# Scores of the second attention in a two-layer kernel: 32-key instead of 64-key tiles on the matmul array

## The chip, the cores and the metric

The kernel runs on one core of a Trainium2 chip. The metric is the time of one execution on the device, in microseconds (us); 1 us is 1000 nanoseconds (ns). Before the change it takes 3774.46 us, the median of three runs (3773.48 to 3776.23). The profiled execution, from which all views below are taken, spans 3772.0 us.

Names of the engines: PE is the matmul engine, PEld its loading of weights (the stationary operand of a matmul, which is loaded by an instruction of its own), DVE the vector engine, ACT the scalar engine with the exponentials, POOL the general-purpose engine, SP the engine that starts most transfers. SBUF is the on-chip memory, PSUM the small memory that matmuls write to[...].

## What is computed

The input x has 16 images of 256 channels by 32 x 32 positions, so 1024 positions ("tokens") of 256 channels for each image. Two layers follow each other, all in fp32.

The first is a self-attention with 4 heads of width 64, an output projection and a residual. The second is a transformer block: group norm, self-attention with 8 heads of width 32 and a projection, a residual, group norm again, and an MLP from 256 to 1024 channels and back with a GELU.

The part that matters here is the second attention, cut to its core:

```python
q, k, v = qkv[0], qkv[1], qkv[2]                  # each (B, 8 heads, 1024, 32)
attn = jnp.einsum('bhnd,bhmd->bhnm', q, k) * scale + phys_bias
attn = jax.nn.softmax(attn, axis=-1)
out = jnp.einsum('bhnm,bhmd->bhnd', attn, v)
```

The score of query n and key m is a sum over only 32 products (d). A score matrix has 1024 x 1024 entries for each head and image.

## The kernel before, in words

The kernel goes through the images one after the other. For each it runs attention_a (the first attention), then attention_b (the second), then the two halves of the MLP. What does not depend on the attention that is running, such as the next image's query, key and value products (qk_a, v_a), this image's own (qk_b, v_b), or the second half of the previous image's MLP (tile m, the function reduce), is cut into pieces, and a list `fill` says after which step of attention_b which pieces are issued. So in attention_b the PE's instructions come in a fixed order, written out by the program: a unit of scores, the weighting of the previous unit's exponentials with the values, one or two filler pieces, and again.

**A unit of scores** (function `scores`) belongs to an item i (one block of TB = 512 queries and one group of four heads; four items for each image) and to two blocks of 128 keys (m = 0 and 1). For each of the four heads g and each block of 128 keys it writes a 128 x 512 piece of the transposed scores to PSUM: keys on the partitions, queries along the free axis. The head's 32 channels are the rows of the array that the matmul uses (its contraction), the keys are the columns. A head takes 32 of the 128 rows, so four heads fit above each other. Before the change, the 128 keys are split in two halves of HALF = 64, so a matmul uses a tile of 32 rows by 64 columns, and eight such tiles fill the array. That is 16 matmuls in a unit. The trace records each fp32 matmul as two weight loads and two matmuls, so there are 32 matmul records in a unit, and with 16 images x 4 items x 4 units = 256 units, 8192 records.

**Where scores go.** For m = 0, heads 0 and 1 go to two single PSUM banks (tags b0, b1), and heads 2 and 3 to one "wide" buffer of two banks. For m = 1 two wide buffers are used. There are three wide buffers, handed out in turn, also to the fillers. A buffer is free again when ACT or DVE has read it. ACT takes the exponential of each buffer (line 483), DVE sums the exponentials for the denominators (line 498).

**The weighting** (function `weigh`, line 519) multiplies the values with the exponentials of the previous unit: full 128 keys as contraction, 32 output channels of a head as columns, so a tile of 128 rows by 32 columns, four of which fill the array: 8 matmuls, 16 records. The fillers are issued through `product` (line 279), which in attention_b is set by `cols[0] = D` to the same shape, four column tiles of 128 x 32. The denominators (line 541) have this shape too. So in attention_b the scores alone use another tile shape.

The first attention has scores and weighting in tiles of 64 x 64 (lines 336 and 357), and the first MLP product uses the whole array, 128 x 128 (line 802).

## Time and profile before

| what | value |
|---|---|
| time | 3774.46 us |
| span of the profiled execution | 3772.0 us |
| PE busy | 3757.8 us (100%), 38335 matmul records |
| weight loads (PEld) busy | 1492.0 us (40%) |
| DVE, ACT, POOL busy | 2231.3 (59%), 2034.8 (54%), 78.5 us (2%) |
| granted PE clock | full speed over the span |
| data moved | 78.27 MB, mean 21 GB/s |

A record of a matmul in the profile has a start, which is measured, and an end, which is modelled. Matmuls are pipelined: on different tiles of the array they run at the same time, and the next on the same tile starts before the modelled end of the last. So the time for which a group of matmuls holds the engine is read from the spacing of starts, or from the chain of waits, which follows the work that ended last and gives each stretch of it a length. A record's own duration is longer than that and can't be summed.

In the list of groups, a line has the source line, the engine, the operation, output and inputs by their names, the tile of the array (rows*columns) and shape, the count, then the busy time in us and the mean of one in ns, then the idle time of the engine ahead of it and who ended it.

### The profile page before, as it was taken

Reading aid. Unit: us, or ns where it says so; the run is one execution under the profiler, and the core shown is the slowest. Engines: PE = TensorE matmul, PEld = TensorE weight load, DVE = VectorE, ACT = ScalarE, POOL = GpSimd, SP = SyncE. Lnnn points to the kernel's source line nnn. Section 1 sums busy time; section 2 is a strip of 40 time slices with the busy share of each in tenths; the row PEclk is TensorE's granted clock in tenths of the full one; section 3 lists DMA queues with packets and bytes.
Section 4 is the critical chain, followed back from the end, with each engine's and each line's share of the span. In section 5 each row is a group of like instructions: output and inputs, shape, how many; then the busy total and the mean of one; then the engine's idle time right before and its main releaser. Section 6 shows DMA issues by size and latency. Waiting matters only on the chain.

```text
span 3772.0 us, 86793 instructions
## 1 busy us (share of the span) xinstructions
PE 3757.8 (100%) x38335; PEld 1492.0 (40%) x38335; DVE 2231.3 (59%) x2764; ACT 2034.8 (54%) x2624; POOL 78.5 (2%) x245
## 2 busy tenths in 40 slices
PE   9999999999999999999999999999999999999999
PEld 3334343343433434334343333443334333343335
DVE  4674656656566565665656656565565655646573
ACT  4665546555465554555555455554655546555461
POOL 1000000000000000000000000000000000000000
PEclk9999999999999999999999999999999999999999
DMA  2000000000001000000000000010010100000000
GB/s 85 13 13 13 30 13 16 27 13 30 12 17 32 7 30 13 19 29 9 28 13 23 26 10 33 7 33 15 13 30 7 33 15 13 30 7 22 15 12 22
DMA packets 63052, 78.27 MB, mean 21 GB/s; under 512 B 35820, under 2 KB 37356, under 8 KB 62668
## 3 DMA queue, kind: packets, MB, share of 16 engines
q1 hardware_dynamic: 59964, 71.85, 6.2%
q8 instruction: 302, 4.95, 0.5%
q0 software_dynamic: 400, 0.41, 0.1%
q14 instruction: 82, 0.67, 0.1%
q10 hardware_dynamic: 2304, 0.40, 0.1%
HBM read 54.28 MB, written 17.56 MB: 19 GB/s over the span
## 4 chain that ended last, share of the span: by engine, by line
PE 97%; DVE 1%; issue 1%; ACT 1%; DMA 0%; ACTq 0%; POOLq 0%; POOL 0%; DVEq 0%
PE s_b L468 13%; PE acc_b L519 12%; PE m L802 12%; PE m L279 12%; PE s_a L336 12%; PE acc_a L357 11%; PE qk_b L279 6%; PE qk_a L279 6%; PE o L279 3%; PE v_b L279 3%; PE v_a L279 3%; PE j L279 3%; PE den_b L541 1%; PE den_a L388 1%; DVE es_a L369 0%
## 5 line engine op out<-in xcount | busy, mean ns | idle before, releaser
L483 ACT ACTIVATE e_b<-s_b 128x1024 f32<-128x1024 f32 (+1 forms) x1280 | 982.6, 864 | 471.0 <-PE s_b L468 471.0
L498 DVE TENSOR_TENSOR es_b<-es_b,e_b 128x1024 f32<-128x1024 f32 x768 | 899.9, 1220 | 337.5 <-ACT e_b L483 337.5
L344 ACT ACTIVATE e_a<-s_a 128x1024 f32<-128x1024 f32 x512 | 521.4, 1025 | 359.6 <-PE s_a L336 349.2
L468 PE MATMUL s_b<-q,k 32*64 32x512 f32 x8192 | 535.8, 601 | 4.0 <-DVE res_b L532 3.3
L336 PE MATMUL s_a<-q,k 64*64 64x512 f32 x4096 | 532.6, 593 | 1.1
L357 PE MATMUL acc_a<-e_a,v 64*64 64x512 f32 x4096 | 528.5, 589 | 0.0
L369 DVE TENSOR_TENSOR es_a<-es_a,e_a 128x1024 f32<-128x1024 f32 x384 | 469.3, 1222 | 85.4 <-ACT e_a L344 73.3
L519 PE MATMUL acc_b<-e_b,v 128*32 128x512 f32 x4096 | 492.1, 598 | 0.0
L279 PE MATMUL m<-g,w 128*32 128x256 f32 (+1 forms) x7664 | 464.1, 379 | 0.0
L802 PE MATMUL m<-gn_h,w 128*128 128x512 f32 x1024 | 451.3, 595 | 0.3 <-DVE gn_h L692 0.3
L810 ACT ACTIVATE g<-m,m1b 128x512 f32<-128x512 f32 x256 | 176.0, 687 | 358.2 <-PE m L802 358.2
L279 PEld LDWEIGHTS m<-g,w 128*32 128x32 f32 (+1 forms) x7664 | 276.7, 112 | 216.8 <-issue 41.9
L468 PEld LDWEIGHTS s_b<-q,k 32*64 32x64 f32 x8192 | 174.2, 130 | 288.8 <-issue 147.1
L802 PEld LDWEIGHTS m<-gn_h,w 128*128 128x128 f32 x1024 | 192.2, 190 | 230.6 <-issue 229.8
L357 PEld LDWEIGHTS acc_a<-e_a,v 64*64 64x64 f32 x4096 | 161.9, 133 | 277.5 <-issue 236.1
L336 PEld LDWEIGHTS s_a<-q,k 64*64 64x64 f32 x4096 | 152.6, 133 | 278.1 <-issue 211.7
L519 PEld LDWEIGHTS acc_b<-e_b,v 128*32 128x32 f32 x4096 | 108.5, 109 | 351.1 <-ACT e_b L483 194.7
L532 DVE TENSOR_TENSOR res_b<-res_b,acc_b 128x512 f32<-128x512 f32 x192 | 131.1, 683 | 196.2 <-PE acc_b L519 196.2
L279 PE MATMUL qk_b<-gn_g,wq 128*32 128x512 f32 (+1 forms) x1280 | 234.0, 592 | 0.0
L279 PE MATMUL qk_a<-x,wp 128*32 128x512 f32 (+1 forms) x1856 | 231.3, 592 | 2.1 <-ACT q L715 1.5
L736 DVE TENSOR_TENSOR v<-v_b,eones 128x512 f32<-128x512 f32 x64 | 44.0, 688 | 291.2 <-PE v_b L279 291.2
L498 DVE TENSOR_TENSOR es_b<-e_b,e_b 128x1024 f32<-128x1024 f32 x128 | 150.6, 1218 | 0.0
(121 smaller groups left out, 2096.3 us busy)
## 6 DMA issues: line engine op xcount, KB each, us to landing
rd_a<-row_a SPq DMA_DIRECT2D x64, 256.0 KB
out_dram<-x SPq DMA_DIRECT2D x64, 256.0 KB
rd_b<-row_b SPq DMA_DIRECT2D x252, 64.0 KB
x<-in_x_dram SPq DMA_DIRECT2D x30, 512.0 KB
w<-in_L_conv_mlp_w_dram SPq DMA_DIRECT2D x2, 1024.0 KB
x<-in_x_dram SPq DMA_DIRECT2D x4, 256.0 KB
sp_b<-d_b SPq DMA_DIRECT2D x63, 8.0 KB
row_b<-inv_b SPq DMA_DIRECT2D x63, 8.0 KB
```

What stands on the lines that cost most here:

```text
L279: nc.tensor.matmul(o[sl], w[:, sl], r, **flags)
L336: nc.tensor.matmul(s[h : h + HALF, g, :], kT[g * D : (g + 1) * D, c, kb * P + h : kb * P + h + HALF], qT[g * D : (g + 1) * D, c, t * TB : ...
L344: nc.scalar.activation(e, s, AF.Exp, scale=float(D) ** -0.5)
L357: nc.tensor.matmul(accs[i][h][g * D : (g + 1) * D, :], v[h * HALF : (h + 1) * HALF, kb, c * 2 + g], e[h * HALF : (h + 1) * HALF, g, :], st ...
L369: nc.vector.tensor_add(sums[i], held[i] if kb == 1 else sums[i], e)
L468: nc.tensor.matmul(outs[g][h : h + HALF, :], kT[g * D : (g + 1) * D, c, k0 : k0 + HALF], qT[g * D : (g + 1) * D, c, t * TB : (t + 1) * TB] ...
L483: nc.scalar.activation(to, s, AF.Exp, scale=float(D) ** -0.5)
L498: ins = nc.vector.tensor_add(d, es[n] if kb == 0 else d, es[2 * block + n])
L519: nc.tensor.matmul(acc[g * D : (g + 1) * D, :], v[:, kb + m, c * G + g], es[2 * m + g // 2][:, g % 2, :], start=(m == 0), stop=(m == 1),)
L532: nc.vector.tensor_add(r, r, acc)
L802: nc.tensor.matmul(ps, k["w1"][:, cc, hc * P : (hc + 1) * P], hn[0][:, cc, t * TB : (t + 1) * TB], start=(cc == 0), stop=(cc == CC - 1),)
L810: nc.scalar.activation(g, ps, AF.Gelu, bias=k["m1b"][:, hc : hc + 1])
```

## The change

In `scores`, the loop over the keys of a block steps by D = 32 instead of HALF = 64. Each head's 128 keys are then four tiles of 32 rows by 32 columns instead of two of 32 by 64. Sixteen such tiles fill the array. The column width becomes that of the weighting, the denominators and the fillers around it; the rows stay 32.

```diff
                 for g in range(G):
-                    for h in range(0, P, HALF):
+                    for h in range(0, P, D):
                         k0 = (kb + m) * P + h
                         nc.tensor.matmul(
-                            outs[g][h : h + HALF, :],
-                            kT[g * D : (g + 1) * D, c, k0 : k0 + HALF],
+                            outs[g][h : h + D, :],
+                            kT[g * D : (g + 1) * D, c, k0 : k0 + D],
                             qT[g * D : (g + 1) * D, c, t * TB : (t + 1) * TB],
```

The written matmuls of a unit go from 16 to 32, the records from 32 to 64 (8192 to 16384 in the kernel), each with a weight load of half the columns. The output buffers, their order, the exponentials and all else are as before; one blank line is gone, so in the changed file the lines after it have numbers lower by one.

## The prediction

> **What bounds the kernel now.** I read the engine totals first, then the chain of waits (what ended last, followed back), then the groups.

> ```profile
> PE 3757.8 (100%) x38335; PEld 1492.0 (40%) x38335; DVE 2231.3 (59%) x2764; ACT 2034.8 (54%) x2624; POOL 78.5 (2%) x245
> PE 97%; DVE 1%; issue 1%; ACT 1%; DMA 0%; ACTq 0%; POOLq 0%; POOL 0%; DVEq 0%
> L468 PE MATMUL s_b<-q,k 32*64 32x512 f32 x8192 | 535.8, 601 | 4.0 <-DVE res_b L532 3.3
> L519 PE MATMUL acc_b<-e_b,v 128*32 128x512 f32 x4096 | 492.1, 598 | 0.0
> ```

> PE is 97% of the chain, so whatever lengthens or shortens PE's own pace in attention_b goes into the span nearly one to one, and DVE and ACT have room. The scores of the second attention are PE's largest group. The chain in order of time, over one ordinary stretch of attention_b, shows what they really cost:

> ```profile
> 347.76 1.72 PE qk_b L279 x16
> 349.48 1.72 PE qk_a L279 x16
> 351.19 1.90 PE s_b L468 x32
> 353.10 1.85 PE acc_b L519 x16
> 354.95 0.86 PE den_b L541 x8
> 355.81 3.45 PE m L279 x64
> ```

> Columns are start, length, and records. Fillers of 128x32 tiles, four at a time, take 1.72 us for 16 records, so four rounds of 0.429 us. A score unit is also four rounds (32 records on eight tiles), yet takes 1.90; the weighting after it is four rounds and takes 1.85. The 0.86 of den_b, two rounds, is again at pace. So what is lost lies where the tile shape changes: 1.90 + 1.85 - 8 x 0.429 = 0.32 us in each of 256 units, about 81 us of the kernel. The weight loads of this unit show part of where:

> ```profile
> 351.12 0.23 PEld L468 LDWEIGHTS s_b<-q,k 32*64 32x64 f32 x16 [0.84 <-issue]
> 351.61 0.15 PEld L468 LDWEIGHTS s_b<-q,k 32*64 32x64 f32 x4 [0.25 <-issue]
> 352.00 0.21 PEld L468 LDWEIGHTS s_b<-q,k 32*64 32x64 f32 x12 [0.24 <-ACT k L715]
> 353.03 0.16 PEld L519 LDWEIGHTS acc_b<-e_b,v 128*32 128x32 f32 x8 [0.81 <-ACT e_b L483]
> ```

> The 16 loads of the unit's first two rounds come in one burst. In the trace's single records they, and the matmuls behind them, start 6.7 ns apart from tile to tile, and the eighth tile starts 47 ns after the first and keeps that lag in every later round. Between stages of one shape the next load instead starts with the last matmul of the round before.

> From the starts of single records a smooth unit (194 of 256 last at most 1.907 us from its first matmul to that of the weighting) adds up as: 93 ns beyond a round from the filler's last matmul to the first score; a first round of 480 instead of 429, since its weights are not loaded ahead; three rounds of 429; 47 for the eighth tile; 517 from the last score to the first weighting, 88 beyond a round; and in the weighting a first round of 453, so 24 too long. The stretched first rounds show in the durations by tile (minimum, median, maximum):

> ```profile
> L468 PE MATMUL s_b<-q,k x8192: 587/587/639, 125.8 to 3681.3; 32*64 32x512 f32 x200
> L519 PE MATMUL acc_b<-e_b,v x4096: 592/592/617, 132.4 to 3691.8; 128*32 128x512 f32 x196
> ```

> 52 ns for 64 columns, 25 ns for 32.

> [...] The trace agrees: 88 to 93 ns extra at each change, none between 128x32 stages. It shows changes of columns alone (128x128 to 128x32: 93) and of both, none of rows alone. [...] Nothing here shows sixteen; eight run here.

> **The change part by part.**

> *Rounds: nothing.* 64 records on sixteen tiles are four rounds, as 32 on eight were. All four tiles of a head now stream the same queries, each for itself. Four streams from the same partitions is what the weighting and the fillers do at 0.429 already.

> *First round of a unit: shorter.* Its load has 32 columns, so the weighting's +24 replaces +51: -27 ns.

> *Sixteen tiles instead of eight: longer.* The last tile starts 15 x 6.7 = 100 ns after the first instead of 47, every later round keeps it, and the weighting, behind a change of shape, waits for the last: +53 ns. No other work fills it.

> *Changes of shape: as before.* 32x32 and 128x32 still differ in rows, so I keep both drains (93 and 88) and the weighting's 24.

> *Waits: none added.* The order of instructions on every engine and the number of waits on PE stay as they were. For m = 1 the second pair of heads waits for its buffer: 352.00 in the view, released by ACT, 33 ns ahead of the matmul that needs it. Its due time moves by -27 (first round) and +27 (it is now the ninth tile, 54 ns, not the fifth, 27), so not at all. Behind such a load stand the rest of the unit, the weighting and the fillers.

> *Supply of instructions: nothing, within a bound.* A unit needs 128 instructions in 1.72 us, one in 13.4 ns; the trace shows sustained 26.8 (16 in 429) at most. But where PE's queue was held by a wait for ACT, its next semaphore instruction follows ACT's end by 57 ns with 8 instructions between, 69 with 16 and 117 with 32: 1.4 to 3 ns each. The cost lies between 0 and, if 26.8 were a ceiling, 128 x 26.8 - 1716 = 1.7 us a unit, 439 us in all. I take 0, since the burst shows the queue to be fast.

> *Sum:* -27 + 53 = +26 to 27 ns in a smooth unit, 194 x 27 = 5.2 us. In the 62 others PE waits for ACT within the unit and only the lag behind the wait counts, some 13 ns: 0.8 us. Together **+6 us: 3780.5 us**, 0.16% slower, and hardly to be told from no change.

> **Rivals.**

> *A, rows alone need no drain, 3730.* If only a change of columns drains, scores and neighbours now run through. That frees 93 + 51 + 88 + 24 = 256 ns a unit, 66 us; with the lag no longer waited for, up to 78. For it: equal columns all through attention_b, and no example of rows alone to refute it. Against it: [...] ACT frees the buffer only 33 ns ahead now, so a unit that begins earlier would wait there. I leave about 45 us: 3730 (3695 to 3750).

> *B, weight loads queue behind each other, 3804.* From the fifth tile on, first-pass loads would meet the second-pass loads of the first tiles (due some 28 ns after the first), each 6.7 ns. Then the sixteenth starts at 27 + 12 x 13.4 = 188 ns, 88 more a unit: 27 + 88 = 115 ns x 256 = 29 us. For it: with eight tiles first-pass loads end (47) before second-pass loads begin (55), so the meeting is untried. Against it: in a unit at 130.5 us whose eighth tile came late, its load starts in the same nanoseconds as another tile's second load, on other rows.

> *C, sixteen tiles don't keep the pace, 3936.* At most 16 matmuls overlap now, 8 ending and 8 begun; with 32 a tile might be held for its recorded 587 ns instead of 429: 4 x 158 x 256 = 162 us. The supply ceiling would give 4213. Against it: [...] the queue's speed.

> **How the numbers follow.** My forecast 0.64, split 0.50 within 0.2% (up to 3782.0) and 0.14 above, since a few ns more a unit pass that line. A 0.12, B 0.16, C 0.08. So faster 0.12, same 0.50, slower 0.38. The range from 3768 to 3818 holds the forecast and B with both signs of a few ns; A and C, 0.20, are left out.

> **What would show it.** In the chain, s_b pieces of 64 records at 1.93 and acc_b still 1.85. In the group of s_b 16384 records with about 542 us busy, maximum duration near 612. In the first burst of weight loads, 32 in about 0.3 us. acc_b at 1.74 and s_b at 1.72 mean A; s_b at 2.0 means B; above 2.2, C. The forecast is wrong if rounds of sixteen are not 0.429 apart, if the lag is not 100, or if a drain vanishes.

## The result, and the profile after

| kernel | time, median of four runs | ratio to before |
|---|---|---|
| before, 64-key tiles | 3774.51 us (3773.48 to 3776.23) | 1 |
| after, 32-key tiles | 3864.47 us (3862.95 to 3866.36) | 1.0238, 95% interval 1.022 to 1.0256 |

The change makes the kernel 90 us slower. The forecast was 3780.5 us, in a range up to 3818: the loss is fifteen times the 6 us that it foresaw. From the page after the change, engine totals, the chain's shares, and the two groups of the second attention:

```profile
PE 3851.3 (100%) x46527; PEld 1544.0 (40%) x46527; DVE 2232.9 (58%) x2764; ACT 2043.4 (53%) x2624; POOL 78.4 (2%) x245
PE 98%; DVE 1%; ACT 0%; DMA 0%; issue 0%; SPq 0%; ACTq 0%; POOLq 0%; POOL 0%; DVEq 0%
L467 PE MATMUL s_b<-q,k 32*32 32x512 f32 x16384 | 628.5, 598 | 1.3 <-DVE res_b L531 1.1
L518 PE MATMUL acc_b<-e_b,v 128*32 128x512 f32 x4096 | 492.1, 598 | 0.0
```

The weighting's group is the same to the tenth, 492.1 us. The score group grew from 535.8 to 628.5. The chain over an ordinary stretch (start, length, records) shows the price of one unit:

```profile
355.01 1.72 PE qk_b L279 x16
356.72 1.72 PE qk_a L279 x16
358.44 2.33 PE s_b L467 x62
360.77 1.85 PE acc_b L518 x16
362.62 0.86 PE den_b L540 x8
363.48 3.45 PE m L279 x64
366.94 2.33 PE s_b L467 x62
369.26 1.85 PE acc_b L518 x16
```

Fillers, denominators and weighting keep their lengths; a score unit goes from 1.90 to 2.33. The 0.43 looks like a fifth round of 0.429, and it is tempting to stop there. It is not a round, as the second of these units shows in order of time (start, length, instructions, and in brackets the engine's idle time ahead of them and its releaser):

```profile
366.87 0.25 PEld L467 LDWEIGHTS s_b<-q,k 32*32 32x32 f32 x32 [0.41 <-issue]
366.87 2.40 PE L467 MATMUL s_b<-q,k 32*32 32x512 f32 x64
...
367.32 0.10 PEld L467 LDWEIGHTS s_b<-q,k 32*32 32x32 f32 x1 [0.21 <-issue]
367.75 0.60 PEld L467 LDWEIGHTS s_b<-q,k 32*32 32x32 f32 x31 [0.32 <-issue]
...
369.19 0.16 PEld L518 LDWEIGHTS acc_b<-e_b,v 128*32 128x32 f32 x8 [0.84 <-ACT e_b L482]
```

The first key block's 32 loads come in one burst of 0.25 us, sixteen tiles deep. Then **one** load of the second block comes, and then nothing; the other 31 begin only 0.43 us later and take 0.60 us. (The first of these is the same tile's second load; the next tile's come 187 ns behind it.) The idle time ahead of them is marked "issue": no semaphore released them. Starts of single records, medians over 255 units, in ns after the unit's first record, a weight load, say it exactly; nearly nine units in ten are within 2 ns of these:

| | first pass, tile 1, 2, ... last | second pass |
|---|---|---|
| block 1 (sixteen tiles) | 2, 8, ... 88 (14th), 103, 120 | 455 ... 571 |
| block 2 | 884, **1078**, 1094, 1111, 1153, ... 1363 | 1313, 1528, ... 1813 |
| weighting | 2330 | |

Block 1 is as forecast. In block 2 the first tile is on time (455 + 429), and the second is 187 ns late; from there on tiles follow each other by 16.5 ns, with two steps of 42 (ahead of the fifth and the ninth tile), instead of 6.7.

The kernel's sum closes with this: (2329 - 1902) x 256 units = 109 us, less the waits inside the units, which fell from 35.0 to 15.8 us (62 units above the smooth length before, 18 after), leaves 90 us, all of the difference.

### The profile page after: what moved, and what is told of

Its sections match the earlier page's. It is cut to its first block, busy times and chain, and to the rows that moved or that the text cites. A ratio compares the mean times of both kernels' runs of the same rounds, so it can differ in the third digit from the quotient of the medians.

```text
span 3864.5 us, 103177 instructions
## 1 busy us (share of the span) xinstructions
PE 3851.3 (100%) x46527; PEld 1544.0 (40%) x46527; DVE 2232.9 (58%) x2764; ACT 2043.4 (53%) x2624; POOL 78.4 (2%) x245
## 4 chain that ended last, share of the span: by engine, by line
PE 98%; DVE 1%; ACT 0%; DMA 0%; issue 0%; SPq 0%; ACTq 0%; POOLq 0%; POOL 0%; DVEq 0%
PE s_b L467 15%; PE acc_b L518 12%; PE m L801 11%; PE m L279 11%; PE s_a L336 11%; PE acc_a L357 11%; PE qk_b L279 6%; PE qk_a L279 6%; PE o L279 3%; PE v_b L279 3%; PE v_a L279 3%; PE j L279 3%; PE den_b L540 1%; PE den_a L388 1%; DVE es_a L369 0%; ACT e_a L344 0%
## 5 line engine op out<-in xcount | busy, mean ns | idle before, releaser
L467 PE MATMUL s_b<-q,k 32*32 32x512 f32 x16384 | 628.5, 598 | 1.3 <-DVE res_b L531 1.1
L518 PE MATMUL acc_b<-e_b,v 128*32 128x512 f32 x4096 | 492.1, 598 | 0.0
L279 PE MATMUL m<-g,w 128*32 128x256 f32 (+1 forms) x7664 | 464.0, 379 | 0.0
L279 PEld LDWEIGHTS m<-g,w 128*32 128x32 f32 (+1 forms) x7664 | 276.7, 112 | 216.8 <-issue 71.2
L467 PEld LDWEIGHTS s_b<-q,k 32*32 32x32 f32 x16384 | 225.9, 103 | 320.1 <-issue 191.9
L279 PE MATMUL qk_a<-x,wp 128*32 128x512 f32 (+1 forms) x1856 | 232.7, 593 | 3.8 <-ACT k L714 2.8
L279 PE MATMUL qk_b<-gn_g,wq 128*32 128x512 f32 (+1 forms) x1280 | 234.1, 592 | 0.0
```

The costliest lines, as they stand in the source:

```text
L279: nc.tensor.matmul(o[sl], w[:, sl], r, **flags)
L467: nc.tensor.matmul(outs[g][h : h + D, :], kT[g * D : (g + 1) * D, c, k0 : k0 + D], qT[g * D : (g + 1) * D, c, t * TB : (t + 1) * TB], star ...
L518: nc.tensor.matmul(acc[g * D : (g + 1) * D, :], v[:, kb + m, c * G + g], es[2 * m + g // 2][:, g % 2, :], start=(m == 0), stop=(m == 1),)
```

## The theories

**Rivals:** Q, each group of 32 rows has a limit of its own (sixteen); B, weight loads into the same rows queue behind each other (from the prediction); R and S, each added tile or instruction costs its share; T, only sixteen tiles at once are too many.

## The experiments

**1. Tiles round the heads.**

```diff
-                for g in range(G):
-                    for h in range(0, P, D):
+                for h in range(0, P, D):
+                    for g in range(G):
```

> The changed kernel with its two inner loops exchanged: the sixteen tiles of a key block are issued round the four heads (h outside, g inside), nothing else. In the changed kernel the second key block of a unit starts one matmul 884 ns after the unit's first and the next only at 1078, then one each 16.5 ns with 42 ns at each fourth; a unit takes 2329 ns. Theory W (TensorE has at most 64 instructions between the oldest unfinished and the newest taken up; a block of sixteen tiles at two passes is 64): the order inside a block is indifferent, one matmul at 884, the next at 1078, unit about 2330, time 3864 +- 6; if the 42 ns at each fourth belong to a change of head rather than to each sixteen instructions, the spread grows to 15 x 42 ns and the unit to 2.7 us (3950). Theory Q (each group of 32 rows has such a limit of its own, sixteen instructions): four matmuls of the second block start near 884-904, twelve are late, unit about 2280, 3852. Theory B (weight loads into the same rows queue behind each other, forecast as a rival): neighbours in order now lie in different rows, so most of the loss goes, 3785-3800.

Measured 3866.94 us, ratio to before 1.025 (1.0233 to 1.0267). Again one matmul of block 2 starts at 884 and the next at 1078, and the unit takes 2329. Q wanted four on time, B wanted the loss gone; both fall.

The steps of 42 ns are not at each fourth tile, as this expectation says. The changed kernel has two, ahead of block 2's fifth and ninth tile; here there are again two, ahead of the fourteenth and fifteenth (after 1261 and 1303). The trace shows what they go with. By the numbering a tile of block 2 takes the place of the tile before it in block 1, and a longer step comes where that tile's second matmul raises the semaphore on which ACT waits (the last matmul into its buffer): tiles 4 and 8 of block 1 in the changed kernel, 13 and 14 here. The longer steps of experiments 6, 7 and 9 stand by the same rule, some 26 ns each. No run changes the semaphores and nothing else, so this is a reading of the traces and not a test.

**2 to 4. Some heads cut, others not.** A list of widths for each head replaces the loop, for instance in the run with eighteen tiles:

```diff
-                    for h in range(0, P, HALF):
+                    h = 0
+                    for w in (D, D, D, D) if (m, g) == (0, G - 1) else (HALF, HALF):
...
-                            outs[g][h : h + HALF, :],
+                            outs[g][h : h + w, :],
...
+                        h += w
```

> The kernel before (two 64-key tiles for each head), but in the first key block of a unit the last head's second tile is cut into two of 32 keys: 17 tiles a unit instead of 16. W: the window of 64 instructions from the first tile's second matmul on still holds the loads of tile 17, so next to nothing is lost: unit 1.90-1.92 us, time 3774-3780. Theory R (each added 32-key tile costs its share of the loss, 351/16 = 22 ns a unit): 3780. Q: as W, 3775-3780.  W and R part in the next run.

> As the run with seventeen, but both tiles of that head are cut: 18 tiles a unit (ten in the first key block, eight in the second). W: the eighteenth tile enters only when the second tile of the first block is finished (462 to 488 + 587 = 1049 to 1075 ns after the unit's first matmul), so its first matmul starts near 1080 instead of 960 and everything after waits for it: unit 2.03-2.09 us, +0.13 to +0.18, time 3800-3815. R: two added tiles, 2 x 22 ns x 256 = 3786. Q: only the head that has four tiles meets its limit, in the second block it has two: 3775-3785.

> The kernel before, but the first of the four heads alone is cut into four 32-key tiles, in both key blocks: 20 tiles a unit. W: tiles 18 to 20 are late (the last three of the last heads), last first-pass matmul near 1110-1137, unit 2.11-2.14 us, 3815-3830. Q: the first head's second tile of the second block is late and holds the eight behind it in the order, unit about 2.25 us, 3840-3850. R: four added tiles, 4 x 22 x 256 = 3797.

Measured 4050.0 (1.0732, 1.0714 to 1.075), 4048.28 (1.0727, 1.0709 to 1.0745) and 4316.95 us (1.1434, 1.1415 to 1.1453): every theory missed by far, because I had taken for granted that tiles of two widths run side by side. They don't. From the chain of the run with seventeen tiles:

```profile
345.43 3.06 PE s_b L468 x34
348.49 1.85 PE acc_b L520 x16
...
353.79 3.06 PE s_b L468 x34
```

Between the last 64-column matmul (522 ns) and the first 32-column one (1039) lie 517 ns, 88 beyond a round, and again 518 from 1499 back to 2017; the two rounds of the odd tiles stand alone. 32x64 and 32x32 differ in columns alone, 32x32 and the weighting's 128x32 in rows alone, and both give 517. These runs tell nothing of W or R.

**5 and 6. The same 128 instructions in two orders.** To change the number of instructions and keep the width, each 64-key matmul is cut into two of 256 queries. In the first of the two runs the loop over halves q stands outside those over g and h, in the second inside:

```diff
+                for q in range(2):
                     for g in range(G):
                         for h in range(0, P, HALF):
...
-                            qT[g * D : (g + 1) * D, c, t * TB : (t + 1) * TB],
+                            qT[g * D : (g + 1) * D, c, q0 : q0 + TB // 2],
...
```

> The kernel before with its two 64-key tiles for each head, but every score matmul cut into two of 256 queries; in a key block all first halves are issued, then all second halves. Instructions of a unit as many as in the changed kernel (128 in two passes), tile width as before. Theory W (at most 64 TensorE instructions between the oldest unfinished and the newest taken up): the oldest halves finish early (about 267 + 373 = 640 ns after the unit's first matmul) and hand their places on, the second block starts on time near 910, unit 1.89-1.93 us, 3772-3785. Theory S (twice the instructions cost the loss by themselves, by supply): 3850-3880.

> The same instructions in another order: the two halves of a tile follow each other, tile after tile. W: the first tile's second half is the oldest unfinished from about 640 to 1068 ns and the window reaches from it to the first tile of the second block only, so that block's other seven tiles start from about 1090 on, 25-35 ns apart, instead of 918-958; unit 2.25-2.35 us, 3850-3875. S: as in the run with the halves apart, 3850-3880 in both or 3774 in both.

Measured **3777.90** us, 1.001 (1.0004 to 1.0017), and **3872.17** us, 1.0258 (1.0241 to 1.0275). The groups and one piece of each chain, halves outside first:

```profile
L469 PE MATMUL s_b<-q,k 32*64 32x256 f32 x16384 | 532.7, 382 | 11.4 <-DVE res_b L533 6.9
354.56 1.91 PE s_b L469 x64
```

```profile
L469 PE MATMUL s_b<-q,k 32*64 32x256 f32 x16384 | 637.6, 386 | 1.6 <-DVE res_b L533 1.6
358.04 2.36 PE s_b L469 x61
```

As many instructions of the same form, and 94 us between them from order alone. With the halves outside, the first halves are finished from 268 + 374 = 642 ns on, and block 2 starts at 916. With the halves inside, the first tile's last matmul starts at 700 and is finished at 1074; block 2's first tile starts at 916, its second at 1109, loaded 31 ns after 1074. S falls: what counts is how long the oldest stays. The late tiles follow at 33 ns for eight instructions (59 at two of the steps), so 4.1 ns each, as 16.5 for four in the changed kernel.

**7. Two heads of block 1 in halves.**

```diff
                     for h in range(0, P, HALF):
                         k0 = (kb + m) * P + h
-                        nc.tensor.matmul(
-                            outs[g][h : h + HALF, :],
...
+                        for q in range(0, TB, TB // (2 if m == 0 and g >= 2 else 1)):
+                            q1 = q + TB // (2 if m == 0 and g >= 2 else 1)
+                            nc.tensor.matmul(
+                                outs[g][h : h + HALF, q:q1],
...
```

> The kernel before, but only the last two heads of the first key block have their four matmuls cut into halves, each pair in succession: 48 instructions in that block instead of 32 (80 a unit). W: from the first tile's second matmul on the window holds the second block's first five tiles; the last three start from about 1100 instead of 945-958; unit 2.08-2.14 us, 3812-3832. S (loss in proportion to the added instructions, 16 of 64): unit +0.107, 3796-3802. No loss at all (3774) would speak against W's place in the order.

Measured 3822.54 us, 1.0128 (1.0111 to 1.0145). Block 2's tiles start at 911, 918, 924, 931, 943, then 1104, 1147 and 1163: five on time and three late, as numbered. A piece of its chain:

```profile
353.53 2.16 PE s_b L469 x32
355.69 1.85 PE acc_b L520 x16
```

The unit, 2157 ns, is a little over the 2.14 expected, by a step of 43 ns (1104 to 1147) that I hadn't counted. A share for each instruction would have been 2.01.

**8. One tile of 128 keys for each head**, the other direction:

```diff
-                    for h in range(0, P, HALF):
+                    h = 0
+                    for w in (P,):
...
-                            outs[g][h : h + HALF, :],
-                            kT[g * D : (g + 1) * D, c, k0 : k0 + HALF],
+                            outs[g][h : h + w, :],
+                            kT[g * D : (g + 1) * D, c, k0 : k0 + w],
...
```

> One 128-key tile for each head instead of two of 64: 32 instructions a unit. The opposite direction of the change. By the steps of the forecast: the first round's stretch grows from 52 to about 105 ns with the load, the lag of the last tile falls from 47 to 20 ns: unit 1.91-1.94, 3772-3790. W has nothing to say against it (no block fills the window): same. If tiles of 128 columns did not run beside each other, 3.4 us or more a unit (over 4150).

Measured 3780.68 us, 1.0018 (1.0009 to 1.0027), unit 1929 ns. Its durations (minimum, median, maximum) and a piece of its chain:

```profile
L468 PE MATMUL s_b<-q,k x4096: 587/587/692, 128.9 to 3691.3; 32*128 32x512 f32 x196
339.50 1.93 PE s_b L468 x16
```

The first round is 533, so stretched by 104, and the last tile is 20 behind. The forecast's way of summing held here, since nothing fills.

**9 to 12. Fewer heads, one width.** Back in the changed kernel's own shape, scores, exponentials and sums of some heads are left out, and other heads' exponentials take their place in the weighting, so PE's other work stays. For three heads:

```diff
-                for g in range(G):
+                for g in range(G - 1):
                     for h in range(0, P, D):
...
-                        es[2 * m + g // 2][:, g % 2, :],
+                        es[2 * m + g // 2][:, g % 2 if g < 3 else 0, :],
```

For two heads the loop ends at G // 2, only the first of the two exponential buffers of a block is made, and all four heads are weighted from it. The companions step h by HALF.

> The changed kernel (32-key tiles), but of the four heads of a unit only three get scores, exponentials and sums; the fourth is left out and weighted with the third's exponentials. Twelve tiles a key block, 48 instructions. Theory W (at most 64 instructions between the oldest unfinished and the newest taken up): the second block's first five tiles are in the window and start on time (884 to 911 ns after the unit's first matmul), the other seven from 1078 on, 16.5 ns apart with one or two steps of 42; the last at 1203-1230, unit 2.17-2.20 us, 3825-3850. Theory T (only sixteen tiles at once are too many; twelve keep the pace): unit 1.90, within 5 us of the run with 64-key tiles and three heads, 3745-3778.

> The companion: the kernel before (64-key tiles) with the same head left out, six tiles a key block, 24 instructions. Both theories: nothing late, the last tile 33 ns behind the first instead of 47, unit 1.89 us; fewer waits for ACT, since it has an eighth less to do there: 3745-3773.

> The changed kernel (32-key tiles) with scores, exponentials and sums of two heads only; the other two are left out and weighted with the first two's exponentials. Eight tiles a key block, 32 instructions, so both blocks of a unit fit into 64. W and T: nothing late, eight tiles start 884 to 931, unit 1.875-1.885 us (24 for the first load, 47 for the eighth tile, 88 for the change of shape, four rounds), 3730-3770. If 32-column tiles lose something by their shape, not by their number: unit over 1.95.

> The companion: the kernel before (64-key tiles) with the same two heads left out, four tiles a key block. The steps of the forecast alone part it from the run with 32-key tiles: +27 for the wider first load, -27 for the four tiles fewer (20 ns of lag instead of 47). W and T: unit 1.875-1.885, times of the two runs within 4 us of each other. This is the forecast's sum, +26 at eight against sixteen tiles, taken where the window can't bind.

| heads, tile | time | ratio to before | unit, ns |
|---|---|---|---|
| three, 32 keys | 3819.08 | 1.012 (1.0104 to 1.0137) | 2171 |
| three, 64 keys | 3752.77 | 0.9945 (0.9928 to 0.9961) | 1889 |
| two, 32 keys | 3744.63 | 0.9925 (0.9909 to 0.9942) | 1876 |
| two, 64 keys | 3743.31 | 0.9923 (0.9906 to 0.994) | 1876 |

Chain pieces of three heads at 32 keys, then of two:

```profile
349.60 2.17 PE s_b L467 x48
351.77 1.85 PE acc_b L521 x16
```

```profile
352.08 1.88 PE s_b L467 x32
353.96 1.85 PE acc_b L518 x16
```

With twelve tiles a block, five tiles of block 2 start at 884, 891, 898, 904 and 911, the other seven at 1078 to 1204. That refutes T, and again number 67 is in and 69 out. With eight tiles the 32-key tile loses nothing, and it ties with its companion as the forecast's terms of +27 and -27 have it. So the shape as such is not slow here, and eight tiles more in a unit cost nothing, against R. The whole time of the twelve-tile run was 6 us under what I expected although its unit was right: the two three-head kernels differ by 70.3 us in their score units (567.4 against 497.2 us) and by 66.3 us in time; where the other 4 us went wasn't traced.

No version that computes all the scores beat the kernel before. It has eight tiles a block, two blocks fit the window, and its rounds already stand 0.429 apart.

## Why the prediction was wrong, point by point

- **The step that failed: "Rounds: nothing", and with it "Supply of instructions: nothing, within a bound".** I asked how fast instructions come, not how many may be under way. By W, sixteen tiles of four instructions use up the window, so from its second tile on block 2 waits for block 1's records to end (587 ns after their start), not merely for its tiles to be free (429 later). In the sum, 1928 forecast against 2329: +187 for the wait of block 2's second tile; +191 because the fifteen late tiles then spread over 1363 - 1078 = 285 ns instead of 14 x 6.7 = 94; +21 because their second pass comes 450 later and not 429, a first round's stretch once more; 2 of rounding. The supply of 1.4 to 3 ns an instruction was also too fast: once places came free, the tiles followed at 4.1 ns an instruction, and at two steps 26 ns later than that. The bound of 439 us did contain the answer, but I put it at 0 and left no case in between.
- **Rival C named the outcome (s_b above 2.2) but not the cause.** Tiles are not held for 587 ns: second passes start 453 after the first in block 1. By W only the instructions' places are held that long, and that costs once a unit, not in each round. That sixteen tiles keep the pace was my estimate: before the change the scores have eight at once.
- **Rival A is refuted** by 517 ns from 32x32 scores to 128x32 weighting: a change of rows alone costs the same 88 beyond a round. The trace before has no change of rows alone; that both drains (the prediction's word for the 93 and 88 ns) would stay was my estimate. **Rival B is refuted** by block 1's burst and by the first experiment.
- **Right:** the first round (455 - 2 = 453; longest matmul forecast near 612):

```profile
L467 PE MATMUL s_b<-q,k x16384: 587/588/613, 128.3 to 3773.8; 32*32 32x512 f32 x200
```

  Right too: the 93 and 88 at the changes of shape kept (from a filler of 512 columns to the first score 522 to 523 ns in both kernels, from the last score to the weighting 517 to 518), acc_b at 1.85, 32 loads in 0.25 us where about 0.3 was forecast. The lag was 116 to 118 instead of 100, since the 15th and 16th tile followed by 12 to 17 ns.
- **Misread, and not foreseen, in the change's favour:** the waits inside the units fell by 19 us. The prediction has PE waiting for ACT in the 62 units above the smooth length; by the trace 52 of these waits end on DVE and six on ACT alone. In 28 of them the third head of block 2 waited 0.42 us for its buffer, 11.9 us in all, as here before the change:

```profile
408.01 0.21 PEld L468 LDWEIGHTS s_b<-q,k 32*64 32x64 f32 x8 [0.24 <-DVE x L825]
```

  In the longer units of the changed kernel none of these 28 is left.
- **In the prediction's list of a smooth unit,** the 517 ns contain the last of the three rounds, and the 93 lie ahead of the unit: 480 + 3 x 429 + 47 + 88 = 1902.

## What to carry to other kernels

When a change multiplies small matmuls, count instructions under way as well as rounds. Each fp32 tile has four here, and the runs fit a window of 64 or 65 that moves on only when its oldest instruction has ended (the next load came 31 ns after the recorded end). Cutting the tiles smaller cost nothing here while two successive blocks fitted (two heads, 3744.63 against 3743.31 us); where they don't fit, issue first what finishes early, as the two orders of the halves show (3778 against 3872 us). The sign in this profile was a weight load that waited for "issue" in the middle of a stage, with no semaphore to release it.

## What was not expected of the hardware

- The next load follows 31 ns after the recorded end of the oldest matmul: 1042 to 1073 (changed kernel), 1074 to 1105 (halves inside), 1069 to 1100 (two heads in halves). The ends are modelled, but the records last 587, 374 and 587 ns, and the three agree, which speaks for taking the end as the moment when a place comes free. Whether the limit counts 64 instructions or 32 pairs of load and matmul is open, as every matmul here brings its load.
- Tiles of two widths, 32x64 and 32x32, don't run side by side: 517 ns from the last start of one to the first of the other, and a unit with seventeen tiles took 3.06 us.
- The first round's stretch grows with the columns loaded: 24, 52 and 104 ns for 32 (changed kernel), 64 (before) and 128 columns (one tile of 128 keys). A load's record lasts 104, 131 and 184 ns in the median for these three widths, each with 32 rows.
